# A selective scan whose partitions hold pairs of channels by states, with scaled copies read straight from PSUM and one buffer per pair

## The chip, the cores and the metric

The kernel runs on one core of one Trainium2 chip. The time is the device time of that core in microseconds: 16271.34 is the median of three runs before the change, which lie between 16253.17 and 16275.21. TensorE, VectorE, ScalarE and GpSimd are called PE, DVE, ACT and POOL in the profile, and SP is the engine from whose queue every DMA of this kernel is issued.

## What is computed

Two images of 256 x 256 pixels with 128 channels go through two layers, each of which adds its result to its input. The first is a group norm and an attention along one image axis with an output projection. The second, where nearly all of the change lies, is a group norm and a selective scan over the L = 65536 pixels of an image, for 256 inner channels d and 16 states n:

```python
xz = x @ in_proj_w.T;  xi, z = split(xz)           # 256 channels each
xs = silu(depthwise_conv3x3(xi))                   # (B, 256, L)
dts, Bs, Cs = rows of einsum(xs, x_proj_w)         # 8, 16 and 16 rows
delta = softplus(dt_w @ dts + dt_b);  A = -exp(A_logs)
h[d, n] = exp(delta[d] * A[d, n]) * h[d, n] + (delta[d] * xs[d]) * Bs[n]   # along L
y[d] = sum over n of h[d, n] * Cs[n]  +  Ds[d] * xs[d]
out = (layernorm(y) * silu(z)) @ out_proj_w.T
```

All data are float32.

## The kernel before the change

The attention runs first and writes its result `x1` to DRAM. Then comes the scan, in 128 steps: 64 for each image, each of four rows of pixels, so T = 1024 positions. Within a step a *unit* is one scan instruction on 128 partitions and 1024 positions. The 128 partitions are 32 channels by 4 states, so 256 channels by 16 states are 32 units (`NU = 32`). The partition of channel c and state r is 4c + r. `PAIRS` lists the 16 pairs of units in their order as half h of the channels, group m of four states, and first channel group q.

A unit needs four things. Its decay is `exp(delta * A)` on ACT (line 1237), where `delta_r` is a spread of 32 rows of delta over the 128 partitions, read back from DRAM (`spread`, line 1154; five buffers). Its drive is `du * B` on POOL, for the two units of a pair in one instruction of 2048 elements (line 1244), from `du_r`, another spread (two buffers), and `bb`, four rows of B repeated over the channels (`repeat`, line 1149). Its scan is on DVE (line 1275). After it, the last column is kept as the state for the next step (`remember`, lines 1282 and 1284, ACT), the result is multiplied by `cc`, the repeated C, and the sums over states are matmuls with the 0/1 matrix `sel` (`add_up`, line 1325). The multiplication is on DVE for 16 units (`product`, line 1292) and on POOL for the eight pairs in `POOLED` (`products`, line 1297).

The eight units of the last group of states (m = 3, `TURNED`) get their drive in another way. PE transposes delta times xs so that positions are on partitions (`turn_du`, line 965, into the PSUM tile `ut_ps`), ACT copies this into `zt` (`turn_du_out`, line 972, two of the eight blocks of 128 positions at a time), then makes the four states' versions of it by copies scaled by B (`drives`, line 976), and PE transposes each unit's 128 columns back (`turn_in`, line 1263) into PSUM. `zt` is laid out as block, channel, state: the fourth state's place takes the unscaled copy, every copy steps over four floats as it reads and writes, and the fourth is scaled in place and last.

PSUM has two buffers for decays, `da0` and `da1`, two banks for the running sums y, and two single banks, called p and f, through which pass all projections of the next step and the closing rows of the last one. SBUF has six buffers `work0` to `work5` of 2 x 1024 per partition, called rooms. A pair in `POOLED`, or of the turned ones, holds a room from its drive to its sum. For a pair whose products are on DVE, the drive's room is given back after the scan, and the product takes another (`work`, `open_pair`, `product`). The decay goes to PSUM, or, for turned units, to the room.

The order is written out by hand. `TIMES` gives each piece of work a time in units of a scan, relative to its step, and `at` and `at_time` collect the pieces of all steps, sort them by time and issue them so. The times only order: each engine runs its instructions in that order, and an instruction waits for those it depends on. The projections of a step carry times from about -47 on, more than one step ahead of its scans, and its closing rows (`finish_row`) up to 71. SP's queue, with the fetches, is ordered in the same way. A DMA that waits for a buffer holds up those behind it.

Of the kernel before, what the change touches and what calls it, by code (L numbers as in the profile page):

```python
# [22 lines left out]
def attn_then_ssm_kernel(  # L23
# [86 lines left out]
    for k in range(2):  # L110
# [37 lines left out]
    NQ = P // CQ  # L148
    NCG = DI // CQ
# [4 lines left out]
        sel, ident.rearrange("p (c r) -> p c r", r=SR), AX.X, ALU.add  # L154
# [4 lines left out]
    with tc.tile_pool(name="prep", bufs=1) as prep, tc.tile_pool(  # L159
# [30 lines left out]
        alog_d = dram.tile([CQ, SR, NCG, NSG], F32, name="alog_d")  # L190
        for g in range(NCG):
            for m in range(NSG):
                nc.sync.dma_start(
                    out=alog_d[:, :, g, m],
                    in_=A_logs[g * CQ : (g + 1) * CQ, m * SR : (m + 1) * SR],
                )
        alog = prep.tile([P, NCG, NSG], F32, name="alog")
        nc.sync.dma_start(out=alog, in_=alog_d.rearrange("c r g m -> (c r) g m"))
# [119 lines left out]
    with ExitStack() as actx:  # L318
# [268 lines left out]
        with tc.manual_schedule(engines=engines):  # L587
# [71 lines left out]
    POOLED = (2, 4, 10, 12, 18, 20, 26, 30)  # L659
    SUMS = ((0, 2), (4, 6), (8, 10), (12, 14), (16, 18), (20, 22), (24, 26), (28, 30))  # L660
    TIMES = {
        "add_up": (6.724, 10.523, 15.234, 17.357, 23.577, 27.066, 31.528, 34.187,),
        "begin": (-46.647,),
        "conv": (-37.319, -33.26, -30.256, -23.187,),
        "conv_out": (-37.203, -32.298, -29.079, -22.531,),
        "decay": (
            -0.457, -0.009, 1.46, 2.524, 2.97, 3.951, 4.748, 6.603, 7.256, 7.99, 7.7, 8.96, 9.084,
            7.786, 12.346, 13.841, 15.488, 16.811, 17.403, 14.296, 19.264, 20.338, 21.36, 21.952,
            23.923, 24.277, 25.955, 26.637, 26.688, 28.054, 29.215, 30.729,
        ),  # L670
        "drive": (
            -2.478, -0.654, 1.762, 3.81, 6.989, 11.716, 14.121, 17.755, 19.949, 23.283, 25.806,
            26.998,
        ),
        "drives": (
            -8.898, -8.755, 2.16, 8.854, -5.671, -4.828, -5.842, -1.931, -5.258, 3.165, -5.885,
            6.474, 2.13, 5.925, -3.57, 1.156,
        ),
        "fetch_b": (-4.274, -3.132, 4.233, 5.726, 22.495,),
        "fetch_c": (-2.23, 2.972, 5.721, 10.592, 28.034,),  # L680
        "fetch_cx": (-6.513,),
        "fetch_delta": (-9.068, -2.243, 0.347, -2.618, 11.064, 13.651, 5.759, 10.856,),
        "fetch_du": (-5.916, -3.021, 10.561, 13.429,),
        "gate": (-33.667, -30.07, -30.491, -26.072,),
        "gate_out": (-33.279, -28.439, -30.401, -25.691,),
        "inner": (-40.499, -39.775, -36.487, -34.84, -31.681, -31.179, -27.674, -24.89,),
        "inner_out": (-39.934, -39.214, -35.665, -34.411, -31.186, -30.784, -27.39, -23.412,),
        "load": (-52.341,),
        "normalise": (-43.293, -42.071,),
        "product": (  # L690
            0.814, 1.744, 6.726, 7.428, 8.79, 9.803, 15.226, 15.302, 17.41, 17.593, 23.225,
            23.505, 24.863, 25.246, 28.32, 29.93,
        ),
        "products": (5.397, 7.89, 14.546, 17.263, 21.546, 22.117, 27.902, 34.092,),
        "remember": (
            1.264, 2.345, 3.214, 6.053, 6.484, 7.988, 9.009, 9.1, 11.486, 14.169, 14.492, 15.761,
            17.254, 17.474, 20.057, 21.886, 23.549, 23.215, 25.088, 26.351, 27.149, 29.047,
            30.658, 32.752,
        ),
        "row_back": (41.992, 49.875, 57.857, 65.191,),  # L700
        "row_fetch": (43.062, 45.977, 52.544, 63.797,),
        "row_gated": (44.51, 49.95, 58.115, 65.232,),
        "row_leave": (45.329, 51.392, 61.182, 70.675,),
        "row_mix": (44.946, 51.011, 60.158, 69.774,),
        "row_norm": (41.251, 49.16, 55.004, 63.737,),
        "row_scales": (41.007, 47.422, 54.441, 63.428,),
        "row_stats": (39.857, 46.949, 53.374, 62.217,),
        "row_turn": (39.103, 45.623, 53.215, 61.229,),
        "silu": (-20.93,),
        "size": (-17.158, -16.246, -14.523, -14.865,),  # L710
        "size_out": (-16.533, -15.379, -13.973, -14.754,),
        "softplus": (-12.917,),
        "start_up": (-5.227, 19.105,),
        "start_up_y": (6.598, 23.449,),
        "states": (-20.725, -18.696,),
        "states_out": (-19.252, -17.616,),
        "times": (-11.031,),
        "turn": (-44.119, -42.473,),
        "turn_b": (-13.925,),
        "turn_b_out": (-12.571,),  # L720
        "turn_du": (-9.691, -6.021, -7.213, -4.676,),
        "turn_du_out": (-9.002, -5.843, -7.087, -4.562,),
        "turn_in": (9.374, 10.415, 10.881, 11.321, 17.974, 18.627, 19.701, 20.235,),
        "y_out": (20.647, 36.827,),
# [17 lines left out]
    LAST = TIMES["y_out"][NH - 1] + 0.1  # L742
# [23 lines left out]
    for i, piece in enumerate(pieces):  # L766
        at_time(i - 2.5, piece)

    def project(k):
# [23 lines left out]
        def begin():  # L793
            if s == 0:
                if k > 0:
                    nc.gpsimd.memset(xn[:, 0, :], 0.0)
                first = s1.tile([P, WT, C], F32, name="ob")
                nc.sync.dma_start(
                    out=first, in_=x1[b][0].rearrange("(t p) c -> p t c", p=P)
                )  # L800
# [624 lines left out]
```

## Time and profile before

| what | value |
|---|---|
| median of three runs | 16271.34 us |
| time of the profiled execution | 16262.75 us |
| its span, first to last instruction | 16261.0 us |
| mean granted PE clock | 0.926 |
| busy: PE, DVE, ACT, POOL | 84%, 84%, 85%, 78% |
| one step, from the 128 starts of silu (2550.3 to 16050.2 us) | 106.3 us |
| bytes moved by DMA | 3122 MB, 54.5% of the 16 DMA engines' span on the main queue |
| issues of `delta_r` and of `du_r` | 1024 each, of 512 KB, landing in 6.2 and 6.3 us |

A row of the groups reads: line, engine, operation, output and inputs by the program's names, shapes, count; then busy time in us and the mean of one in ns; then how long the engine was idle just before, and what ended that. A row of waits reads: who waited for whom, us in all, how many times, the longest. A row of the table of stretches gives, for a stretch of time, the busy time of every engine, the granted PE clock, the share of DMA and GB/s. A `SPq` row of the timeline is the issue of a DMA: its start, and how long SP took to issue it.

### The profile page before, as it was taken

To read this page: it belongs to the slowest core of one execution; us is meant where nothing else is said; L and a number is where in the kernel's file an instruction comes from. 1 tells how busy PE (TensorE), PEld (TensorE's weight loads), DVE (VectorE), ACT (ScalarE), POOL (GpSimd) and SP (SyncE) were. 2 spreads that over 40 slices of the span, in tenths; PEclk is the share of its full clock that TensorE was granted. 3 is DMA by queue.
4 is the path that set the end of the run, shared out by engine and by line. 5 is a ranking of instruction groups with operands and counts; after the bars stand their busy time and mean duration, and the time that the engine had idled before them with its cause. 6 is when DMAs were issued, how large, how long until landed. Compare 5 with 4: busy or idle time off the path is not lost.

```text
span 16261.0 us, 265160 instructions
## 1 busy us (share of the span) xinstructions
PE 13681.8 (84%) x102443; PEld 8025.9 (49%) x102443; DVE 13663.5 (84%) x11479; ACT 13899.9 (85%) x24467; POOL 12670.3 (78%) x2960
## 2 busy tenths in 40 slices
PE   6999997888888888888888888888888888888887
PEld 5877884444444444444444444444444444444444
DVE  6665556888888888888888888888888888888888
ACT  3555557999999999999999999999999999999997
POOL 1111115999999999989899999999999989999988
PEclk9999998999999999999999999999999999999998
DMA  4322224565655666555666556665556566566664
GB/s 189 135 84 88 84 83 153 209 213 206 212 209 207 212 213 208 208 206 209 211 208 211 209 205 213 213 209 207 207 208 216 202 209 209 208 212 208 212 209 168
DMA packets 1336402, 3122.11 MB, mean 192 GB/s; under 512 B 108856, under 2 KB 700256, under 8 KB 1314656
## 3 DMA queue, kind: packets, MB, share of 16 engines
q1 hardware_dynamic: 1335136, 3105.15, 54.5%
q8 instruction: 804, 13.17, 0.3%
q14 instruction: 462, 3.78, 0.1%
HBM read 2416.88 MB, written 687.88 MB: 191 GB/s over the span
## 4 chain that ended last, share of the span: by engine, by line
ACT 44%; PE 24%; DVE 8%; issue 5%; DMA 1%; POOL 1%; SPq 0%; POOLq 0%; DVEq 0%; ACTq 0%
ACT zt L976 14%; ACT da L1237 10%; DVE work L1275 7%; PE y L1325 5%; PE u_ps L851 4%; PE dt_ps L916 4%; ACT work L1237 3%; ACT raw L844 3%; ACT zt L972 3%; PE o_ps L1104 2%; PE da L1263 2%; PE xi_ps L835 2%; ACT sz L891 2%; PE yt L1053 2%; PE xd_ps L898 1%
## 5 line engine op out<-in xcount | busy, mean ns | idle before, releaser
L1244 POOL TENSOR_TENSOR work<-du_r,bb 128x2048 f32<-128x2048 f32 x1536 | 7163.3, 4679 | 793.6 <-DVE da L1275 409.9
L1275 DVE TENSOR_TENSOR_SCAN da<-da,state,work 128x1024 f32<-128x1024 f32 x2048 | 4776.2, 2344 | 256.2 <-ACT da L1237 216.9
L1237 ACT ACTIVATE da<-delta_r,a_neg 128x1024 f32<-128x1024 f32 x3072 | 3430.6, 1119 | 82.0 <-DVE work L1275 47.4
L976 ACT ACTIVATE zt<-zt,bt 128x256 f32<-128x256 f32 x4096 | 3073.1, 787 | 37.6
L1292 DVE TENSOR_TENSOR work<-da,cc 128x1024 f32<-128x1024 f32 x2048 | 2465.1, 1219 | 495.7 <-ACT state L1282 261.4
L1275 DVE TENSOR_TENSOR_SCAN work<-da,state,work 128x1024 f32<-128x1024 f32 x1024 | 2388.8, 2343 | 478.8 <-ACT da L1237 469.7
L1297 POOL TENSOR_TENSOR work<-work,cc 128x2048 f32<-128x2048 f32 x512 | 2350.9, 4592 | 419.0 <-ACT state L1284 415.0
L851 PE MATMUL u_ps<-raw,w_cv 128*32 128x255 f32 (+1 forms) x24576 | 1819.8, 456 | 896.3 <-ACT raw L844 337.4
L1275 DVE TENSOR_TENSOR_SCAN work<-work,state,da 128x1024 f32<-128x1024 f32 x1024 | 2346.4, 2333 | 158.0 <-PE da L1263 132.6
L1297 POOL TENSOR_TENSOR work<-work,ccx 128x2048 f32<-128x2048 f32 x512 | 2318.3, 4552 | 19.1 <-ACT state L1284 17.8
L1325 PE MATMUL y<-work,sel 128*32 128x512 f32 x16384 | 2204.0, 641 | 15.0 <-POOL work L1297 15.0
L851 PEld LDWEIGHTS u_ps<-raw,w_cv 128*32 128x32 f32 x24576 | 864.8, 128 | 1867.3 <-ACT sz L891 434.9
L475 POOL TENSOR_TENSOR x1g<-xc,bo_all 128x512 f32<-128x512 f32 x256 | 316.2, 1276 | 1843.9 <-DVE stats L530 1835.8
L835 PE MATMUL xi_ps<-xn,w_in 128*32 128x256 f32 x16384 | 1164.9, 392 | 342.9 <-ACT raw L844 325.9
L425 ACT ACTIVATE e<-s_ps,nmx 128x256 f32<-128x256 f32 x1024 | 477.2, 476 | 970.1 <-DVE nmx L416 877.0
L1263 PE MATMUL da<-ident,zt 128*128 128x128 f32 x8192 | 1179.0, 291 | 25.5 <-ACT state L1282 22.0
L1237 ACT ACTIVATE work<-delta_r,a_neg 128x1024 f32<-128x1024 f32 x1024 | 1163.4, 1148 | 2.0 <-PE y L1325 0.3
L1325 PEld LDWEIGHTS y<-work,sel 128*32 128x32 f32 x16384 | 561.7, 115 | 1208.4 <-issue 1059.0
L1263 PEld LDWEIGHTS da<-ident,zt 128*128 128x128 f32 x8192 | 975.9, 149 | 326.1 <-DVE work L1275 107.5
L1053 PE MATMUL yt<-centre,ys 128*128 128x256 f32 x4096 | 1010.5, 390 | 127.3 <-ACT ob L1121 127.2
L835 PEld LDWEIGHTS xi_ps<-xn,w_in 128*32 128x32 f32 x16384 | 500.3, 111 | 1025.2 <-ACT raw L844 504.1
L1053 PEld LDWEIGHTS yt<-centre,ys 128*128 128x128 f32 x4096 | 738.2, 190 | 477.8 <-ACT ob L1121 285.8
(175 smaller groups left out, 22878.7 us busy)
## 6 DMA issues: line engine op xcount, KB each, us to landing
delta_r<-delta_d SPq DMA_DIRECT2D x1024, 512.0 KB, 6.2
du_r<-du_d SPq DMA_DIRECT2D x1024, 512.0 KB, 6.3
bb<-bc_d SPq DMA_DIRECT2D x640, 512.0 KB, 6.8
cc<-bc_d SPq DMA_DIRECT2D x640, 512.0 KB, 4.7
sz_d<-sz SPq DMA_DIRECT2D x128, 1024.0 KB, 4.1
xs_d<-xs SPq DMA_DIRECT2D x128, 1024.0 KB, 7.5
delta_d<-sz SPq DMA_DIRECT2D x128, 1024.0 KB, 5.0
du_d<-xs SPq DMA_DIRECT2D x128, 1024.0 KB, 6.2
```

The lines of the kernel that those rows point to most:

```text
L835: nc.tensor.matmul(o["xi", j][r * CQ : (r + 1) * CQ, q, :], w_in[:, h, c : c + CQ], xn[:, i * RB + r, :], start=True, stop=True,)
L851: nc.tensor.matmul(o["u"][q * CQ : (q + 1) * CQ, r, a:z], w_cv[:, h * NQ + q, r, dx, :], o["xin"][:, q, a + dx - 1 : z + dx - 1], start=(i ...
L916: nc.tensor.matmul(o["dt"], w_dt[:, h, :], o["xd"][0:DR, i * TB : (i + 1) * TB], start=True, stop=True,)
L976: nc.scalar.activation(v["zt"][:, j, :, r], v["zt"][:, j, :, SR - 1], AF.Copy, scale=v["bt"][:, j, r : r + 1],)
L1053: nc.tensor.matmul(o["yt"][:, j, :], ys[k, h][:, t0 + j * P : t0 + (j + 1) * P], centre[:, (1 - h) * P : (1 - h) * P + DI], start=(h == 0) ...
L1237: nc.scalar.activation(da, spreads["delta", k, h, q], AF.Exp, scale=a_neg[:, g, m : m + 1])
L1244: nc.gpsimd.tensor_tensor(open_pair(t, time_of(k, "drive", DRIVEN.index(t % NU))), spreads["du", k, h, q], repeat_of("bb", t).unsqueeze(1) ...
L1263: nc.tensor.transpose(da[:, j * P : (j + 1) * P], given[k]["zt"][:, j, a : a + CQ, :].rearrange("p c r -> p (c r)"), ident,)
L1275: nc.vector.tensor_tensor_scan(u["h"], u[ins[0]], u[ins[1]], st, ALU.mult, ALU.add)
L1292: nc.vector.tensor_tensor(u["yc"], u["h"], repeat_of("cc", t), ALU.mult)
L1297: nc.gpsimd.tensor_tensor(hb, hb, repeat_of("cc", t).unsqueeze(1).to_broadcast([P, 2, T]), ALU.mult)
L1325: nc.tensor.matmul(y[q * CQ : (q + 1) * CQ, cols], sel, units[u]["yc"][:, cols], start=False, stop=last,)
```

## The change

Five things change together.

- The partitions of a unit: channel c = 2a + b and state r now lie on partition 8a + 2r + b, so that two neighbouring channels are neighbours (`CB = 2`). `sel`, `a_neg`, the repeats of B and C and `zt` follow. `zt` becomes block, pair of channels, state, channel of the pair. The small DRAM tile `bc_d` holds each row of B and C twice.
- A spread becomes two transfers, one for even and one for odd partitions, of 64 partitions each.
- `turn_du_out` goes. `drives` reads `ut_ps` in PSUM, for all four states, and writes pairs of floats into `zt`.
- A pair keeps one room from its drive (or decay) to its sum; the DVE product overwrites the drive.
- Unit 30's product and state no longer go with unit 31's on POOL: 31 is multiplied on DVE (17 products in place of 16), 30 on POOL alone (`single`).

Beside that, the gating multiply of a closing row is issued in two halves, the first row of an image is normalised after the others, the group scales of the second image are computed ahead of the first step, the closing rows of the last step are ordered one unit later, and every time in `TIMES` is new.

```diff
-        sel, ident.rearrange("p (c r) -> p c r", r=SR), AX.X, ALU.add
+        sel.rearrange("p (a b) -> p a b", b=CB),
+        ident.rearrange("p (a r b) -> p a b r", r=SR, b=CB),
+        AX.X,
+        ALU.add,
...
-    POOLED = (2, 4, 10, 12, 18, 20, 26, 30)
+    POOLED = (2, 4, 10, 12, 18, 20, 26)
+    SINGLES = (30,)
...
         "drive": (
-            -2.478, -0.654, 1.762, 3.81, 6.989, 11.716, 14.121, 17.755, 19.949, 23.283, 25.806,
-            26.998,
+            -0.913, -0.273, 0.924, 3.225, 7.461, 10.178, 10.839, 19.277, 21.727, 16.814, 25.326,
+            27.843,
         ),
         "drives": (
-            -8.898, -8.755, 2.16, 8.854, -5.671, -4.828, -5.842, -1.931, -5.258, 3.165, -5.885,
-            6.474, 2.13, 5.925, -3.57, 1.156,
+            -9.769, -9.422, -8.809, -9.524, -7.004, -6.997, -6.999, -7.229, -5.886, -3.425,
+            -5.126, -5.754, -4.723, -4.106, -3.106, -2.068,
         ),
...
-        "fetch_delta": (-9.068, -2.243, 0.347, -2.618, 11.064, 13.651, 5.759, 10.856,),
-        "fetch_du": (-5.916, -3.021, 10.561, 13.429,),
+        "fetch_delta": (-2.633, -1.452, -1.361, -10.151, 10.962, 10.988, 10.844, 15.649,),
+        "fetch_du": (-4.933, -1.787, 10.579, 10.708,),
...
-                v["bc"] = dr.tile([2 * NS, T], F32, name="bc_d")
+                v["bc"] = dr.tile([2 * NS, CB, T], F32, name="bc_d")
...
-        def turn_du_out(i):
-            if i == 0:
-                v["zt"] = s6.tile([P, T // P, DI, SR], F32, name="zt")
-            nc.scalar.copy(v["zt"][:, 2 * i : 2 * i + 2, :, SR - 1], o["ut", i])
-
         def drives(j, n, m):
+            if (j, n) == (0, 0):
+                v["zt"] = s6.tile([P, T // P, DI // CB, SR, CB], F32, name="zt")
             for r in range(n, m):
                 nc.scalar.activation(
-                    v["zt"][:, j, :, r],
-                    v["zt"][:, j, :, SR - 1],
+                    v["zt"][:, j, :, r, :],
+                    o["ut", j // 2][:, j % 2, :].rearrange("p (a b) -> p a b", b=CB),
                     AF.Copy,
                     scale=v["bt"][:, j, r : r + 1],
                 )
...
     def spread(k, name, tl, h, q):
-        nc.sync.dma_start(
-            out=tl,
-            in_=given[k][name][h, q * CQ : (q + 1) * CQ, :]
-            .unsqueeze(1)
-            .to_broadcast([CQ, SR, T]),
-        )
+        rows = given[k][name][h, q * CQ : (q + 1) * CQ, :]
+        for j in range(CB):
+            nc.sync.dma_start(
+                out=tl[j:P:CB, :],
+                in_=rows[j:CQ:CB, :].unsqueeze(1).to_broadcast([CA, SR, T]),
+            )
...
-            hb = work(now, summed(t) if pooled(t) else t + 1)
+            hb = work(now, done(t))
             for i in range(2):
-                units[t + i].update({"pair": hb, "hb": hb[:, i, :], "yc": hb[:, i, :]})
+                units[t + i].update({"pair": hb, "hb": hb[:, i, :]})
...
     def product(t):
         u = units[t]
-        if t % 2 == 0:
-            yc = work(time_of(t // NU, "product", KEPT.index(t % NU)), summed(t))
-            for i in range(2):
-                units[t + i]["yc"] = yc[:, i, :]
-        nc.vector.tensor_tensor(u["yc"], u["h"], repeat_of("cc", t), ALU.mult)
+        nc.vector.tensor_tensor(u["hb"], u["h"], repeat_of("cc", t), ALU.mult)
+
+    def single(t):
+        u = units[t]
+        nc.gpsimd.tensor_tensor(u["hb"], u["h"], repeat_of("cc", t), ALU.mult)
```

## The prediction

> **What bounds the kernel now.** I read the page first (every working engine is 78 to 85% busy, so no share names the limit), then the silu rows (line 871), to get one step of the scan loop: its 128 executions start from 2550.3 to 16050.2 us, so a step is (16050.2 - 2550.3) / 127 = 106.3 us, and 128 steps are 13,606 of the 16,261 us span. The attention ahead and the ramps are not changed in anything that counts.
>
> Then busy time in stretches of one step, cut where silu runs (8062) and where the next step's copies begin (8104.3):
>
> ```profile
> core 0: us, PE busy (x) PEld busy (x) DVE busy (x) ACT busy (x) POOL busy (x), PEclk, DMA share, GB/s
> 7998.00:8062.00 64.00, 50.66 (x494) 25.69 (x492) 55.85 (x32) 62.03 (x107) 56.52 (x14) 0.95 0.55 187
> 8062.00:8104.30 42.30, 38.41 (x204) 22.47 (x204) 39.05 (x22) 36.18 (x59) 40.27 (x9) 0.88 0.71 244
> ```
>
> The step has two stages. In the first (64 us) ScalarE is busy 62.03 us and nothing else is over 57: it is the bound. In the second (42.3 us) POOL, DVE and PE are each over 90%, and ScalarE is not. The chain that ended last says the same: from 8034 to 8062 it is ScalarE pieces and their issue alone, many of them of `zt`; after that DVE, then mostly PE.
>
> What VectorE waits for in the first stage:
>
> ```profile
> DVE work L1275 <- ACT da L1237: 3.7, 3, 1.6
> DVE work L1292 <- ACT state L1282: 2.0, 2, 1.5
> DVE da L1275 <- ACT da L1237: 1.6, 2, 1.4
> DVE work L1292 <- DMA cc<-bc_d: 0.5, 1, 0.5
> ```
>
> 7.3 of its 8.15 idle us there end with a ScalarE instruction: the decays and state copies stand behind the `zt` copies in ScalarE's queue. The groups that the change touches:
>
> ```profile
> L1244 POOL TENSOR_TENSOR work<-du_r,bb 128x2048 f32<-128x2048 f32 x1536 | 7163.3, 4679 | 793.6 <-DVE da L1275 409.9
> ...
> L976 ACT ACTIVATE zt<-zt,bt 128x256 f32<-128x256 f32 x4096 | 3073.1, 787 | 37.6
> L1292 DVE TENSOR_TENSOR work<-da,cc 128x1024 f32<-128x1024 f32 x2048 | 2465.1, 1219 | 495.7 <-ACT state L1282 261.4
> ...
> L844 ACT COPY raw<-xi_ps 128x512 f32<-128x512 f32 x1024 | 597.4, 583 | 57.1 <-PE xi_ps L835 51.7
> ...
> L972 ACT COPY zt<-ut_ps 128x512 f32<-128x512 f32 x512 | 550.2, 1075 | 113.5 <-PE ut_ps L965 113.5
> ...
> L1077 ACT ACTIVATE yn<-yt,rstd 128x256 f32<-128x256 f32 x1020 | 425.2, 473 | 0.1
> ...
> L1096 DVE TENSOR_TENSOR yn<-yd,szr 128x512 f32<-128x512 f32 x510 | 343.7, 674 | 167.5 <-PE yd L1088 167.5
> ```
>
> Of these, L976 is 32 and L972 four copies a step: 25.2 + 4.3 = 29.5 us of ScalarE, nearly all in the first stage.
>
> **The change, part by part (us per step).**
>
> *Scaled copies from PSUM, in pairs of channels.* The four copies out of `ut_ps` (L972) go: -4.3. The 32 scaled copies stay, but read contiguous PSUM and write runs of two floats. No row has such a write. Nearest is L1077, the same copy from PSUM with a scale per partition, contiguous: 473 ns. The dearest is a write of single floats 16 bytes apart: L972 against L844, both 512 elements, shows 1075 - 583 = 492 ns more, so 246 for 256 elements: 473 + 246 = 719. Between them: the copies of 1024 (L1335, 1007) and 512 elements (583) give 159 ns fixed and 0.83 per element, so L972's 512 separate writes take (1075 - 159) / 512 = 1.79 each; 128 runs at 1.79 are 229 ns where 256 contiguous elements are 212. That gives 490 ns, and I take it: 32 x (787 - 490) = -9.5. At 719 it would be -2.2, at 473 -10.0. [...]
>
> The bank of `ut_ps` is now held through eight copies (about 4 us by the 490) in place of one of 1.08. Behind it wait the next projections of PE on that bank; PE is busy 50.66 of 64 us there, and this cover takes it. If it did not, some 3 us on each of four turns would stand on PE, and the conv behind them would be late.
>
> *17 products on VectorE.* One product of 1219 ns more, +1.2. The gating multiply is cut in two: 674 ns for 512 and 1219 for 1024 elements give 129 ns fixed, so four more instructions are +0.5. POOL loses half a product of 4592 ns (L1297's row): -2.3. One state copy more on ScalarE, under 0.2.
>
> *One room per pair.* The product is written over the drive's room, so a room is held from the drive to the summing matmuls, not in two shorter holds. Counting holds over the written times, 4.2 of 6 rooms were in use on average and 4.6 will be. POOL's drives wait 410 us in all for a scan to free a room (3.2 a step); that wait turns into one for PE's summing. I put it at 0, because the tightest new hand-over (the drive for unit 16 after the summing of units 4 to 7) has another drive of 4.7 us of POOL ahead of it, while the summing is 16 matmuls (1.7 to 2.5 us where the chain has them). Without that cover it is at most those 2.5.
>
> *Spreads in two transfers.* 16 spreads become 32: 16 DMAs of about 0.55 us of issue on SP, +8.8. SP issued 48 a step in 106 us, so it has the room; what counts is where it stands in order. The trace of the queue:
>
> ```profile
> 8013.26 1.24 SPq L1155 DMA_DIRECT2D du_r<-du_d  x2
> 8021.70 0.38 SPq L1122 DMA_DIRECT2D out_dram<-ob  x1
> 8022.13 1.16 SPq L1155 DMA_DIRECT2D delta_r<-delta_d  x2
> ```
>
> Two `du_r` issues of 1.2 us become four of 2.3, and the `delta_r` behind them start 1.1 to 1.7 later. [...] Who waits: the decays of units 0 to 2 of the next step, issued behind `du_r`, which waits for POOL's last drive. From the end of that drive POOL still does one product and one drive (4.6 + 4.7) before unit 0 can scan, and unit 1 follows 2.34 later, so its decay (1.12) must start at 10.5; SP needs 6 issues (3.5) and 6.2 to land, 9.7. It fits by 0.8 us. Price 0, up to 6 if serialized.
>
> *Everything reordered by the new times.* By these, ScalarE's copies are ended before unit 0 scans and no longer run into units 1 to 8; silu and softplus keep their places beside the turned units. PE's work by stage is the same within 1 us. The group scales of the second image move ahead of the first step, a few us once, beside a load that PE waits for anyway.
>
> **The sum.** First stage: ScalarE falls from 62.0 to 48.2 and VectorE becomes the longest: 55.85 + 1.5 = 57.4 (POOL 56.5 - 2.3). Of its idle time the 7.3 us owed to ScalarE shrink; with ScalarE at some 80% and two decay buffers I leave 1.5, and 0.8 of others: 59.7 for 64.0. Second stage: nothing of its limits is touched, 42.3. Together 102.0, or 4.3 less. Times 128 is 550 us. The profiled execution took 16,262.75 (span 16,261.0), so 15,713; the median of the runs is 8.6 higher: 15,720. A difference under 0.2%, 33 us, could not be told from none.
>
> Own range of this case: with no wait left on ScalarE and DVE at its busy time, and the second stage's POOL work (40.3) with 1.4 of its waits: 58.2 + 41.7 = 99.9, 15,450; with pairs at 719 ns ScalarE still has 55.5 and about half of the waits stay, 104, 15,980.
>
> **Rivals.**
> - *Only the slack moves* (0.14). DVE and POOL wait for each other through rooms and landed halves, and the step keeps some 105: 1.0 to 1.5 a step, 16,090. For it: POOL and DVE sum to 94 and 96 of busy time per step, and today the best engine is 8% under the step. Against: the trace puts the first stage's waits on ScalarE.
> - *The split fetches come late* (0.13, slower). Place: `delta_r` behind four `du_r` on SP, twice a step. If a half lands in 10 us in place of 6.2, the decay is 3 us late each time, and ScalarE's queue behind it too. It decides when lateness is above 4.3 a step; at 10 us for both places it is 6 a step: 108.0, or 1.7 over today's, 16,490. For it: POOL already waits 155 us for `du_r`. Against: ScalarE waits 1.4 us for `delta_r` in the whole run.
> - *The pairs don't speed the copy and VectorE takes what is freed* (0.04): within 0.2%, 16,270.
>
> **Chances.** The main case 0.69, own range 15,450 to 15,980; with the first rival, faster 0.83, same 0.04, slower 0.13. The range from 15,450 to 16,110 leaves out the slow cases, that of no difference, and a little below: under 2 in 10.
>
> **What would show it.** Right: the group of scaled copies from PSUM near 490 ns, no copy row of 512 elements into `zt`; the step near 102; ScalarE near 83 us a step; VectorE's waits for decays and state copies under a third of today's 948 us (469.7 + 216.9 + 261.4 in the whole run). Wrong: `delta_r` or `du_r` among the releasers of decays and drives with over 2 us a step; PE's projections waiting for `zt` copies; copies near 719.

## The result, and the profile after

The changed kernel takes 17,068.77 us (median of four runs, 17,059.38 to 17,074.62), the kernel before 16,262.26 beside it: a ratio of 1.0495, 95% interval 1.0477 to 1.0513. It is 4.95% slower; forecast were 15,720, within 15,450 to 16,110. The profiled execution has a span of 17,064.4 us. A step, from the silu executions on `sz` (2574.0 to 16,856.8 us), is (16,856.8 - 2574.0) / 127 = 112.5 us for 106.3.

From the page of the kernel after: busy times, the main DMA queue (packets, MB, share of the 16 DMA engines' span), the chain that ended last by engine and by line, three groups, and DMA issues with KB and median us from issue to landing. The chain by engine on the page of the kernel before, for comparison, stands first.

```profile
ACT 44%; PE 24%; DVE 8%; issue 5%; DMA 1%; POOL 1%; SPq 0%; POOLq 0%; DVEq 0%; ACTq 0%
```

```profile
PE 13801.8 (81%) x102443; PEld 7769.8 (46%) x102443; DVE 13797.9 (81%) x12119; ACT 12254.1 (72%) x24083; POOL 12369.2 (72%) x2960
...
q1 hardware_dynamic: 1376608, 3122.06, 65.3%
...
DMA 27%; PE 24%; ACT 13%; DVE 7%; POOL 7%; issue 6%; SPq 1%; DVEq 0%; POOLq 0%; ACTq 0%
DMA cc<-bc_d 9%; PE y L1331 8%; DMA sz_d<-sz 7%; DMA du_r<-du_d 7%; POOL work L1250 6%; DVE da L1281 3%; PE dt_ps L927 3%; PE xi_ps L843 3%; DMA xr<-xs_d 3%; DVE work L1294 2%; PE y L1320 2%; PE u_ps L859 2%; ACT da L1243 2%; ACT L770 2%; DVE work L1281 1%
...
L1250 POOL TENSOR_TENSOR work<-du_r,bb 128x2048 f32<-128x2048 f32 x1536 | 7161.5, 4673 | 2071.9 <-PE y L1331 1053.6
L1294 DVE TENSOR_TENSOR work<-da,cc 128x1024 f32<-128x1024 f32 x2176 | 2613.8, 1216 | 678.9 <-DMA cc<-bc_d 651.3
L984 ACT ACTIVATE zt<-ut_ps,bt 128x256 f32<-128x256 f32 x4096 | 1654.2, 515 | 3.7 <-PE ut_ps L976 3.7
...
delta_r<-delta_d SPq DMA_DIRECT2D x2048, 256.0 KB, 7.9
du_r<-du_d SPq DMA_DIRECT2D x2048, 256.0 KB, 6.1
bb<-bc_d SPq DMA_DIRECT2D x640, 512.0 KB, 7.6
cc<-bc_d SPq DMA_DIRECT2D x640, 512.0 KB, 6.7
sz_d<-sz SPq DMA_DIRECT2D x128, 1024.0 KB, 9.8
```

ScalarE gave what was forecast of it: copies of 515 ns, and (13,899.9 - 12,254.1) / 128 = 12.9 us less a step for 13.8 (62.0 - 48.2). But ScalarE has left the chain (13% for 44%), and DMA has entered it (27% for 1%). The queue moves nearly the same bytes as before (3122 MB for 3105), yet its packets take 0.653 x 17,064 = 11,143 us of 16 engines for 0.545 x 16,261 = 8862, a quarter more.

The stretches of one step (columns as in those shown of before). Since the copies and silu have moved against the scans, the cuts are put at scans: from the scan of unit 20 to that of unit 7 of the next step, and on to unit 20. The prediction's cuts of the kernel before lie within 3 us of these scans.

```profile
7986.20:8047.40 61.20, 49.57 (x467) 24.02 (x469) 54.32 (x33) 46.17 (x97) 56.09 (x14) 0.90 0.75 192
8047.40:8095.50 48.10, 39.88 (x244) 21.64 (x240) 40.85 (x26) 38.38 (x65) 38.11 (x9) 0.93 0.72 223
```

In the first stage ScalarE has fallen to 46.17 us of work (48.2 were forecast), yet the stage takes 61.2 us where 59.7 were forecast. The second has grown from some 43 us to 48.1, and PE, DVE and POOL are 79 to 85% busy in it where each was over 90%. The waits say for what; the last of these rows is of the kernel before:

```profile
POOL work L1250 <- PE y L1331: 1053.6, 333, 7.8
DVE work L1294 <- DMA cc<-bc_d: 651.3, 127, 6.5
...
ACT sz L938 <- DMA sz_d<-sz: 529.9, 126, 5.8
...
POOL work L1250 <- DMA du_r<-du_d: 330.4, 112, 15.7
POOL work L1250 <- DMA delta_r<-delta_d: 288.8, 49, 6.7
ACT da L1243 <- DMA delta_r<-delta_d: 266.3, 191, 3.8
```

```profile
DVE work L1292 <- DMA cc<-bc_d: 171.2, 114, 5.3
```

Waits put down to `du_r` and `delta_r` hold up POOL and ACT for 885 us, 6.9 a step; the prediction had put its sign of failure at 2. (POOL's drives do not read `delta_r`, so its row of 288.8 us may stand for another fetch; without it there are 4.7 a step.) And `cc`, which the change to the spreads doesn't touch, holds up DVE for 651 (171 before). One kind of transfer has got slower for all.

### The profile page after: what moved, and what is told of

Its sections match the earlier page's. It is cut to its first block, busy times and chain, and to the rows that moved or that the text cites. A ratio compares the mean times of both kernels' runs of the same rounds, so it can differ in the third digit from the quotient of the medians.

```text
span 17064.4 us, 269148 instructions
## 1 busy us (share of the span) xinstructions
PE 13801.8 (81%) x102443; PEld 7769.8 (46%) x102443; DVE 13797.9 (81%) x12119; ACT 12254.1 (72%) x24083; POOL 12369.2 (72%) x2960
## 4 chain that ended last, share of the span: by engine, by line
DMA 27%; PE 24%; ACT 13%; DVE 7%; POOL 7%; issue 6%; SPq 1%; DVEq 0%; POOLq 0%; ACTq 0%
DMA cc<-bc_d 9%; PE y L1331 8%; DMA sz_d<-sz 7%; DMA du_r<-du_d 7%; POOL work L1250 6%; DVE da L1281 3%; PE dt_ps L927 3%; PE xi_ps L843 3%; DMA xr<-xs_d 3%; DVE work L1294 2%; PE y L1320 2%; PE u_ps L859 2%; ACT da L1243 2%; ACT L770 2%; DVE work L1281 1%
## 5 line engine op out<-in xcount | busy, mean ns | idle before, releaser
L1281 DVE TENSOR_TENSOR_SCAN da<-da,state,work 128x1024 f32<-128x1024 f32 x2176 | 5059.8, 2344 | 1128.6 <-ACT da L1243 538.1
L1294 DVE TENSOR_TENSOR work<-da,cc 128x1024 f32<-128x1024 f32 x2176 | 2613.8, 1216 | 678.9 <-DMA cc<-bc_d 651.3
L1331 PE MATMUL y<-work,sel 128*32 128x512 f32 x16384 | 2676.4, 783 | 23.0 <-POOL work L1303 16.1
L1281 DVE TENSOR_TENSOR_SCAN work<-da,state,work 128x1024 f32<-128x1024 f32 x896 | 2074.4, 2339 | 144.3 <-ACT da L1243 125.5
L1303 POOL TENSOR_TENSOR work<-work,cc 128x2048 f32<-128x2048 f32 x384 | 1757.6, 4577 | 136.6 <-ACT state L1290 136.5
L984 ACT ACTIVATE zt<-ut_ps,bt 128x256 f32<-128x256 f32 x4096 | 1654.2, 515 | 3.7 <-PE ut_ps L976 3.7
L859 PE MATMUL u_ps<-raw,w_cv 128*32 128x255 f32 (+1 forms) x24576 | 1486.9, 391 | 40.3 <-ACT sz L899 13.5
L927 PE MATMUL dt_ps<-xr,w_dt 8*128 8x512 f32 x1024 | 740.6, 810 | 626.1 <-ACT state L1288 431.2
L976 PE MATMUL ut_ps<-ident,xs 128*128 128x128 f32 x2048 | 389.7, 322 | 933.8 <-DVE yn L1104 422.7
L859 PEld LDWEIGHTS u_ps<-raw,w_cv 128*32 128x32 f32 x24576 | 771.9, 113 | 784.4 <-ACT zt L984 151.5
```

The costliest lines, as they stand in the source:

```text
L859: nc.tensor.matmul(o["u"][q * CQ : (q + 1) * CQ, r, a:z], w_cv[:, h * NQ + q, r, dx, :], o["xin"][:, q, a + dx - 1 : z + dx - 1], start=(i ...
L927: nc.tensor.matmul(o["dt"], w_dt[:, h, :], o["xd"][0:DR, i * TB : (i + 1) * TB], start=True, stop=True,)
L984: nc.scalar.activation(v["zt"][:, j, :, r, :], o["ut", j // 2][:, j % 2, :].rearrange("p (a b) -> p a b", b=CB), AF.Copy, scale=v["bt"][:, ...
L1281: nc.vector.tensor_tensor_scan(u["h"], u[ins[0]], u[ins[1]], st, ALU.mult, ALU.add)
L1294: nc.vector.tensor_tensor(u["hb"], u["h"], repeat_of("cc", t), ALU.mult)
L1303: nc.gpsimd.tensor_tensor(hb, hb, repeat_of("cc", t).unsqueeze(1).to_broadcast([P, 2, T]), ALU.mult)
```

## The experiments

Of two readings, the first is that a spread in two transfers is late because there are more transfers, or because of where they stand in SP's order. The second is that something in the form of the transfers makes each packet slower. A number from the packet records of the traces tells these apart: every run moves 606,208 packets of 4096 bytes, some 442,000 of which are spreads and repeats. Their mean time was 183 ns before and 236 after. Runs of different groups have kernels before of 16,262 to 16,293 us beside them, so they are compared to 0.2% at best.

### One transfer again, and two of other shapes

In a1, a4 and b1 each partition of a spread gets another channel's delta and `du`, so they are of use for their time alone; a2 and a3 give every partition what the kernel before does.

a1, the changed kernel with spreads in one transfer:

```diff
-        rows = given[k][name][h, q * CQ : (q + 1) * CQ, :]
-        for j in range(CB):
-            nc.sync.dma_start(
-                out=tl[j:P:CB, :],
-                in_=rows[j:CQ:CB, :].unsqueeze(1).to_broadcast([CA, SR, T]),
-            )
+        nc.sync.dma_start(
+            out=tl,
+            in_=given[k][name][h, q * CQ : (q + 1) * CQ, :]
+            .unsqueeze(1)
+            .to_broadcast([CQ, SR, T]),
+        )
```

> The changed kernel with each spread as one transfer of 128 partitions, as before the change (each partition then gets the delta and du of another channel, so this is for time alone). Stride theory (partitions two apart make each packet slower) and number theory (32 transfers in place of 16 fill the queue): 15,650 to 15,950, mean time of the 4096-byte packets back from 236 to about 185 ns. Order theory (the new times and the one room per pair keep the engines waiting, the transfers only show it): 16,900 to 17,070.

15,904.75, ratio 0.9751 (0.972 to 0.9781), packets 206 ns: the split of the spreads costs 1164 us of the changed kernel. The packets come only a little more than half of the way back to 183, so something else slows them too.

a2, the kernel before in two transfers, each of all 32 rows for two of the four states; a3, the same in two halves of 16 rows; a4, the changed kernel in two halves; b1, the changed kernel with the form of a2:

```diff
 a2, b1
+        for j in range(2):
+            nc.sync.dma_start(
+                out=tl[j:P:2, :],
+                in_=rows.unsqueeze(1).to_broadcast([CQ, SR // 2, T]),
+            )
 a3, a4
+        for j in range(2):
+            nc.sync.dma_start(
+                out=tl[j * P // 2 : (j + 1) * P // 2, :],
+                in_=rows[j * CQ // 2 : (j + 1) * CQ // 2, :]
+                .unsqueeze(1)
+                .to_broadcast([CQ // 2, SR, T]),
+            )
```

> The kernel before with each spread in two transfers, one for even and one for odd partitions; results unchanged. Stride theory: slower, 16,700 to 17,300, and the 4096-byte packets go from 183 to about 235 ns. Number theory: slower by as much. Order theory: within 100 us of 16,262.

> The kernel before with each spread in two transfers of partitions 0 to 63 and 64 to 127; results unchanged. Stride theory: nearly as before, 16,250 to 16,450, packets near 185 ns. Number theory: like the strided split, 16,700 to 17,300. Order theory: within 100 us of 16,262.

> The changed kernel with each spread in two transfers of partitions 0 to 63 and 64 to 127 (each partition then gets another channel's delta and du, for time alone). Stride theory: 15,700 to 16,100. Number theory: 17,000 to 17,100, as the changed kernel. Order theory: the same 17,000 to 17,100.

> The changed kernel with the split that cost the kernel before only 17 us: each of the two transfers of a spread reads all 32 rows and writes each to two partitions, in place of 16 rows to four (each partition then gets another channel's delta and du, for time alone). Number and order theory (twice the transfers behind the short leads of the new order): 16,950 to 17,150, as the changed kernel. Pattern theory (it is what a transfer reads and where it writes): 15,900 to 16,300, as with one transfer.

a2: 16,302.95, ratio 1.0012 (1.0001 to 1.0022), 186 ns. a3: 16,485.42, 1.0107 (1.0072 to 1.0142), 217 ns. a4: 17,388.94, 1.0661 (1.0628 to 1.0693), 250 ns. b1: 16,008.72, 0.9834 (0.9815 to 0.9854), 206 ns. So b1 has just as many transfers as the changed kernel, in the same order of issue, and is 1060 us faster; two transfers for one cost 104 us (b1 less a1), a tenth of what was lost. The number of transfers falls as the main cause, and with it the late start behind the issues of `du_r`. The stride of the partitions falls too: a2 writes every second partition and is not slower, and a4, which does not, is slower than the changed kernel. With the order alone, a1 would have stayed near 17,000. Of the theories named so far, only that of the pattern, what a transfer reads and where it writes, is left.

b2 is the kernel before with the changed kernel's split (again other channels, for time alone), and d1 the changed kernel with three fetches of delta put behind the stores of `sz_d` and `xs_d` in SP's order, since ACT waits for `sz_d`:

```diff
 b2
+                out=tl[j:P:2, :],
+                in_=rows[j:CQ:2, :].unsqueeze(1).to_broadcast([CQ // 2, SR, T]),
 d1
-        "fetch_delta": (-2.633, -1.452, -1.361, -10.151, 10.962, 10.988, 10.844, 15.649,),
+        "fetch_delta": (-2.633, -1.452, -1.361, -10.151, 11.31, 11.33, 11.29, 15.649,),
```

> The kernel before with the spreads of the changed kernel, two transfers of 16 rows, one to even and one to odd partitions (each partition then gets another channel's delta and du, for time alone). Number and order theory: 16,250 to 16,380, as with the other split in this order. Pattern theory: 16,700 or more.

> The changed kernel with three fetches of delta (times 10.844, 10.962, 10.988) set to 11.29 to 11.33, so that SP issues the two stores of silu, sz_d and xs_d, ahead of these six transfers. Number and order theory: the wait of ScalarE for sz_d (530 us in all) falls under 150 us and the time is 16,400 to 16,900. Pattern theory: within 100 us of 17,069.

b2: 16,444.84, 1.0102 (1.0082 to 1.0122), 209 ns. Its two largest waits for fetches:

```profile
POOL work L1244 <- DMA du_r<-du_d: 453.8, 182, 5.3
DVE work L1292 <- DMA cc<-bc_d: 438.1, 132, 8.0
```

The packets are as slow as the pattern theory has it, but the time is not, 16,445 for 16,700 or more: the same slow transfers cost the kernel before 1% and the changed one some 7%. In b2, POOL and DVE wait 566 us more for `du_r` and `cc` than before, and the time shows 170 of them; the rest takes the place of other waits. Why the new kernel can't do the same is not shown. Its leads are one candidate, and they are mixed: counted from the traces, waits included, the median from a fetch's issue to its first use is 16.8 us before and 11.7 in c1 (a version with the new order, below) for `delta_r`, 11.5 and 9.6 for `du_r`, but 8.6 and 10.9 for `cc`. The other is that ScalarE bounds the first stage of the kernel before and leaves the others slack; no run parts the two. d1: 17,102.87, 1.0506 (1.0485 to 1.0527). `sz_d` lands in 5.7 us for 9.8, and ACT no longer waits for it, but its decays of turned units now wait 603 us for `delta_r` (43 in the changed kernel). This change of order moves the lateness and doesn't mend it.

### The change without its layout of partitions

c1 keeps three of the five parts, copies straight from PSUM in pairs, one room and 17 products, and the new order. It takes back the partition order, the split of the spreads and the doubled `bc_d`. To have pairs all the same, the two channels of a pair are c and c + 128, one of each half h:

```diff
-                v["zt"] = s6.tile([P, T // P, DI // CB, SR, CB], F32, name="zt")
+                v["zt"] = s6.tile([P, T // P, P, SR, NH], F32, name="zt")
...
-                        o["ut", i][:, j, h * P : (h + 1) * P], o["xs"][:, h, t : t + P], ident
+                        o["ut", i][:, j, :, h], o["xs"][:, h, t : t + P], ident
...
-                given[k]["zt"][:, j, a : a + CA].rearrange("p a r b -> p (a r b)"),
+                given[k]["zt"][:, j, q * CQ : (q + 1) * CQ, :, h].rearrange("p c r -> p (c r)"),
```

> The changed kernel with the partitions and the single spreads of before, and still pairs of floats in zt: a pair is a channel and the channel 128 above it, the transposes into ut_ps write every second float, and the transposes out of zt read every second column. Results as the reference's. Number and order theory: 15,800 to 16,000, as with one transfer in the changed kernel (15,905). If the order of the new times were itself the cause: 16,900 or more. If TensorE's strided loads cost much: the transposes into da over 400 ns in place of 279, and 16,000 to 16,400.

15,582.34 (15,574.43 to 15,600.13), 0.9573 (0.9557 to 0.9589): 4.3% faster than before and 8.7% faster than the changed kernel. It beats both. Its page:

```profile
PE 13280.7 (85%) x102443; PEld 7810.3 (50%) x102443; DVE 13763.1 (88%) x12119; ACT 12305.8 (79%) x24083; POOL 12365.0 (79%) x2960
...
q1 hardware_dynamic: 1335136, 3105.15, 56.3%
...
PE 38%; DVE 19%; ACT 12%; DMA 8%; issue 6%; POOL 1%; SPq 0%; DVEq 0%; ACTq 0%; POOLq 0%
...
L1242 POOL TENSOR_TENSOR work<-du_r,bb 128x2048 f32<-128x2048 f32 x1536 | 7168.0, 4683 | 771.9 <-PE y L1322 750.2
...
L1285 DVE TENSOR_TENSOR work<-da,cc 128x1024 f32<-128x1024 f32 x2176 | 2602.1, 1216 | 27.3 <-ACT state L1279 0.7
...
L977 ACT ACTIVATE zt<-ut_ps,bt 128x256 f32<-128x256 f32 x4096 | 1664.2, 514 | 3.8 <-PE ut_ps L969 3.7
```

One of its first stages, by the same scans:

```profile
7949.80:8005.20 55.40, 46.01 (x460) 23.20 (x456) 54.12 (x33) 46.44 (x96) 55.40 (x14) 0.94 0.59 205
```

The wait for `cc` is gone (27 us idle ahead of the products for 679), DMA is 8% of the chain, and a step, from the first and last of softplus's 128 executions on `sz` (2562.5 and 15,409.0), is 101.2 us. The rest of the change is thus worth 693 us (16,275 beside it), some more than the 550 forecast. By stages, as means over 88 steps in us, cut at the scans of units 20, 7 and 20:

| | first | second | step |
|---|---|---|---|
| before | 63.6 | 42.9 | 106.5 |
| forecast | 59.7 | 42.3 | 102.0 |
| c1 | 55.7 | 45.5 | 101.2 |
| changed kernel | 62.4 | 50.3 | 112.8 |

f1 and f2 each put one part of the change back into c1, the doubled repeats and the split of the spreads; f3 takes the pairs from c1 (`zt` as before the change, single floats four apart, but still straight from PSUM):

```diff
 f1
+                v["bc"] = dr.tile([2 * NS, 2, T], F32, name="bc_d")
...
+        rows = given[k]["bc"][a : a + SR].rearrange("r b t -> (r b) t")
+        nc.sync.dma_start(out=tl, in_=rows.partition_broadcast(CQ // 2))
 f2
+        for j in range(2):
+            nc.sync.dma_start(
+                out=tl[j:P:2, :],
+                in_=rows[j:CQ:2, :].unsqueeze(1).to_broadcast([CQ // 2, SR, T]),
+            )
 f3
-                    v["zt"][:, j, :, r, :],
+                    v["zt"][:, j, :, r],
```

> The version with the two halves of the channels as pairs (15,582), with one part of the change put back: bc_d holds each row of B and C twice and a repeat reads eight rows and writes each to 16 partitions, in place of four rows to 32. Partitions get B and C of another state, so it is of use for its time alone. If this pattern of the repeats is what keeps the changed kernel with single spreads 320 us above: about 15,900, packets of 4096 bytes at 206 ns in place of 181, bb and cc landing in 7.6 to 7.8 us in place of 5.8 and 5.9. If those 320 us come from the layout of the pairs or the partition order: about 15,580, packets at 181.

> The same version, with the change's split of the spreads put back: two transfers, each reads every second row, four times, and writes every second partition. The channels go to other partitions, so it is of use for its time alone. If the split's pattern costs what it cost in the changed kernel: 1,000 to 1,200 us more, 16,600 to 16,800, 4 KB packets above 205 ns. If it costs much only together with the doubled repeats: under 400 more, below 15,980.

> The same version, but zt as before (channel, state) and the scaled copies, straight from PSUM for all four states, write single floats with a step of four in place of pairs. By the prediction's upper bound the copy takes 719 ns in place of 514, so ScalarE has 6.6 us more a step in the first stage; that stage was to be 2 us longer, 15,840. If ScalarE is no longer what anything waits for: within 50 us of 15,582. If the copies cost 1075 ns as those of the kernel before did, ScalarE has 18 us more and the step is back above 106: 16,200 or more.

f1: 15,881.74, 0.976 (0.9745 to 0.9774), 206 ns. f2: 16,589.44, 1.0197 (1.0182 to 1.0212), 210 ns. So of the 1486 us between c1 and the changed kernel, the split takes 1007 and the doubled repeats 299, and 180 are left. a1 and f1 have the same transfers and differ in the layout of the pairs and the partitions, and are 23 us apart; so most of the 180 comes when split and doubled repeats are both there. f3: 16,056.70, 0.9872 (0.9856 to 0.9889). Its copies:

```profile
L977 ACT ACTIVATE zt<-ut_ps,bt 128x256 f32<-128x256 f32 x4096 | 2220.8, 739 | 4.5 <-PE ut_ps L969 4.1
```

The pairs are worth 225 ns a copy and 474 us in all, more than the 256 that the prediction's dear case gave (2 us a step); the other parts without them leave about 220.

### What in the transfer makes it slow

All on c1, each changing the spreads alone, and all but g4 with other channels, for time alone. `rows` are 32 rows of one group, or what the slice says:

```diff
 f4  two transfers as in f2, of adjacent rows
+                in_=rows[j * CQ // 2 : (j + 1) * CQ // 2, :].unsqueeze(1).to_broadcast([CQ // 2, SR, T]),
 f5  one transfer, 16 rows, each eight times in succession
+        nc.sync.dma_start(out=tl, in_=rows[0 : CQ // 2].unsqueeze(1).to_broadcast([CQ // 2, 2 * SR, T]))
 f6  one transfer, the same 16 rows in turns
+        nc.sync.dma_start(out=tl, in_=rows[0 : CQ // 2].partition_broadcast(2 * SR))
 g2  one transfer, four rows in turns
+        nc.sync.dma_start(out=tl, in_=rows[0:SR].partition_broadcast(CQ))
 g4  one transfer, the 32 rows, written as 16 pairs
+            in_=rows.rearrange("(a b) t -> a b t", b=2).unsqueeze(2).to_broadcast([CQ // 2, 2, SR, T]),
 g5 (n = 16), g6 (n = 32)  one transfer, all 128 rows of the half, once each
+        nc.sync.dma_start(out=tl, in_=given[k][name][h].rearrange("(i a) t -> a i t", a=n))
```

> The same version with spreads in two transfers to every second partition, but each reads 16 adjacent rows, four times each, in place of every second row; time alone, as the channels go to other partitions. If reading every second row (8 KB apart) is what slows the packets: as the single spread, 15,600 to 15,700 and about 185 ns a packet. If it is that a transfer has only 16 source rows, each read four times: as with every second row, within 100 us of that run and its packets too.

> The version with the halves as pairs, spreads again in one transfer of 128 partitions, but it reads only 16 rows and writes each to eight partitions next to each other; the partitions get other channels, so it is of use for its time alone. If a transfer is slow when it goes over 16 rows in place of 32, whatever the number of transfers: packets of 4096 bytes at 205 ns or more, landing above 7.5 us, time near that of the two transfers, 16,300 to 16,700. If it takes two transfers as well as 16 rows: near the single spread of 32 rows, 15,580 to 15,700, packets at 181 to 185 ns.

> The same 16 rows in one transfer of 128 partitions, but in turns: all 16 rows, then all 16 again, eight times over, as the repeats of four rows are read 32 times over; time alone, for the same reason. If it is the few source rows that slow a transfer: as the run that writes each of 16 rows eight times in succession, within 60 us. If it is the order in which rows and copies are gone through: clearly different from it, and near 15,580 to 15,700 if that one is slow.

> The same version; each spread reads only four rows, in turns, 32 times over, as the repeats do, so the outermost count is 32 and the source rows are fewer than in any other run; the partitions get other channels, so it is of use for its time alone. If the way in which 16 engines share the partitions sets the packets' time: 15,560 to 15,650, packets at 178 to 185 ns. If few source rows slow a transfer: worse than the run with 16 rows eight times each, above 17,000.

> The version with the halves as pairs; each spread reads the same 32 rows in the same order into the same partitions in one transfer, only written down as 16 pairs of two rows, four times each, so that the transfer's outermost count is 16 in place of 32. [...] If the source rows or their number make them slow, or nothing but the data counts: 15,560 to 15,620 and 181 ns.

> The version with the halves as pairs; each spread reads all 128 rows of its half, every row once, as 16 groups of eight rows that lie 16 apart: the outermost count is 16. The partitions get other channels, so it is of use for its time alone. If the outermost count of a transfer (how the DMA engines share the partitions) sets the packets' time: 205 to 240 ns a packet, 16,400 to 17,300. If it is that few rows are read many times: about 15,580 and 181 ns.

> The same 128 rows, each once, into the same partitions, as 32 groups of four rows that lie 32 apart: the outermost count is 32; time alone. If the outermost count sets the packets' time: 178 to 186 ns a packet and 15,520 to 15,650. If the rows, their number or their distance set it: as the run with 16 groups, within 100 us.

f4, 16,657.70, 1.0234 (1.0219 to 1.025): adjacent rows are as slow as every second one, so the distance of the rows isn't it. f5, 17,136.21, 1.0523 (1.0505 to 1.0541): one transfer is slower still than two. f6, 20,534.84, 1.2611 (1.2592 to 1.2629): the same rows in another order, and 3400 us more. g2, 15,523.55, 0.9534 (0.952 to 0.9548): four rows only, and fast, so few rows read often isn't it either. g4, 15,625.49, 0.9588 (0.9572 to 0.9605), tells nothing of this, as the two counts are joined to one of 32 again in the built program; it is c1 a second time, and 0.3% from it. g5 and g6 settle it: the same 128 rows, the same partitions, one transfer, grouped by 16 or by 32. (Which row goes to which partition differs with it: rows read one after the other lie 16 or 32 rows apart. That distance isn't it, as f5, where it is 0 or 1, has packets as slow as g5.) 17,165.13, 1.0538 (1.0522 to 1.0554), against 15,571.34, 0.9566 (0.9549 to 0.9583). From g5's page, the main queue and the spreads' landing, then from g6's:

```profile
q1 hardware_dynamic: 1335136, 3105.15, 62.8%
...
delta_r<-delta_d SPq DMA_DIRECT2D x1024, 512.0 KB, 10.7
du_r<-du_d SPq DMA_DIRECT2D x1024, 512.0 KB, 7.1
```

```profile
q1 hardware_dynamic: 1335136, 3105.15, 56.7%
...
delta_r<-delta_d SPq DMA_DIRECT2D x1024, 512.0 KB, 6.8
du_r<-du_d SPq DMA_DIRECT2D x1024, 512.0 KB, 5.5
```

Same packets, same bytes, 10.7 us for 6.8. All runs in one table, by the outermost count of the transfer's source (the first of the counts that its access pattern goes through in the built program); shares are of the 606,208 packets of 4096 bytes:

| run | spreads | repeats | mean ns | under 170 ns | 280 to 350 ns | us |
|---|---|---|---|---|---|---|
| before | 32 | 32 | 183 | 84% | 4% | 16,262 |
| a2 (order of before) | 2 x 32 | 32 | 186 | 83% | 4% | 16,303 |
| f3 | 32 | 32 | 184 | 86% | 3% | 16,057 |
| c1 | 32 | 32 | 181 | 86% | 2% | 15,582 |
| g4 | 32 | 32 | 181 | 86% | 2% | 15,625 |
| g6 | 32 | 32 | 181 | 87% | 2% | 15,571 |
| g2 | 32 | 32 | 181 | 87% | 2% | 15,524 |
| f1 | 32 | 16 | 206 | 63% | 16% | 15,882 |
| a1 | 32 | 16 | 206 | 63% | 17% | 15,905 |
| b1 | 2 x 32 | 16 | 206 | 65% | 16% | 16,009 |
| b2 (order of before) | 2 x 16 | 32 | 209 | 52% | 9% | 16,445 |
| f2 | 2 x 16 | 32 | 210 | 50% | 6% | 16,589 |
| f4 | 2 x 16 | 32 | 213 | 47% | 7% | 16,658 |
| a3 (order of before) | 2 x 16 | 32 | 217 | 49% | 19% | 16,485 |
| f5 | 16 | 32 | 230 | 44% | 25% | 17,136 |
| g5 | 16 | 32 | 230 | 44% | 25% | 17,165 |
| d1 | 2 x 16 | 16 | 235 | 29% | 23% | 17,103 |
| after | 2 x 16 | 16 | 236 | 28% | 22% | 17,069 |
| a4 | 2 x 16 | 16 | 250 | 27% | 39% | 17,389 |
| f6 | 8 | 32 | 235 | 48% | 20% | 20,535 |

There is no exception: with 32 everywhere the packets take 181 to 186 ns, and with 16 anywhere 206 or more. Counts of spreads and repeats other than 8, 16 and 32 were not run.

f6 has a second loss: its packets take 235 ns, near f5's 230, yet it takes 3400 us more. In its trace exactly eight packets of 4096 bytes are under way during 36% of the time from 5000 to 11,000 us (1.1% in c1, which has 16 for 27%). f6 is the only run with a count of 8; what ties the eight packets to it no run shows.

Why 16 is slow where 32 is fast is not shown either, since the packet records name no engine and no partition: that the engines' shares of the partitions are behind it, as the expectations of g2 and g5 have it, was the author's supposition. What the records show is the packets' times. The median where all counts are 32 is 159 ns, and a1, f1, f5 and g5 have a second heap at 280 to 350, with 16 to 25% of the packets; twice the median is 318. In the changed kernel, with its even and odd halves, most of the slow packets lie between 170 and 280 ns (47% of all), so one doubling does not describe them all.

## Why the prediction was wrong

- **Where it failed: "Spreads in two transfers … Price 0, up to 6 if serialized".** They cost 1007 us on c1, 7.9 a step, and 1164 in the changed kernel. The step reasoned about the start of the transfers (1.1 to 1.7 us later) and took the landing of 6.2 us as given. But the rows of the page that land in 6.0 to 6.3 us, of 64 KB (`bc_d`), 128 KB (`xres`) and 512 KB (`delta_r`), all had another form than the new ones, and that page had rows of 512 KB from 4.7 us (`cc`) to 6.8 (`bb`); that the form of a transfer sets the time of its packets was in no part of the working. Nor did it ask what slower packets do to the others on the same 16 engines: DVE waits 480 us more for `cc` than before.
- **A term left out.** The doubled `bc_d` is named in the change, and the sum has no term for it. It turned the repeats from an outermost count of 32 to one of 16, and cost 299 us.
- **"Up to 6 if serialized"** is a term that no run shows. In its place, the first transfers of `delta_r` and `du_r` in the changed kernel land in 8.2 and 5.8 us (medians from issue to landing), the second in 7.8 and 6.2, where the whole spreads of before took 6.2 and 6.3. Two transfers of 32 groups cost 0.1% in the old order (a2) and some 100 us in the new one (b1 less a1). What costs is the count in each.
- **"It fits by 0.8 us"** was the right place to look, and rested on a landing of 6.2 us. With the 7.9 of the changed kernel the same sum gives 3.5 + 7.9 = 11.4 us for 10.5, and ACT's decays do wait 266 us for `delta_r`. It looked at this one fetch alone; `cc`, `du_r` and `sz_d` are waited for longer.
- **Scaled copies: right.** Taken 490 ns, measured 515 (514 in c1); the upper bound of 719 was measured, with single floats, at 739. The row it went by (1075 ns for 512 single floats four apart, 583 for 512 contiguous) pointed the right way: single floats four apart cost 225 of f3's 739 ns. The held bank: in c1 PE's matmuls wait 190 us for `zt` copies in the whole run (175 of them those of the next turn, 12 the conv), where before they waited 460, so the price of 0 held.
- **17 products, gating halves: not tested alone.** DVE's busy time rose by (13,797.9 - 13,663.5) / 128 = 1.05 us a step for 1.7 forecast, POOL's fell by 2.35 for 2.3.
- **One room per pair: priced 0, and c1 agrees.** The wait for a scan did turn into one for PE's summing, and it is not small (750 us in c1), but the idle time ahead of POOL's drives is 772 us in c1 and was 794. In the changed kernel it is 2072, with the late fetches; the room alone was not undone.
- **The sum.** Without the transfers' forms the step is 101.2 for 102.0 forecast, and the total 15,582 for 15,720, inside the case's own range. That it comes so close is in part luck, as two errors cancel: the first stage fell by 7.9 us for 4.3, and the second, "42.3" and "nothing of its limits is touched", grew by 2.6; why is open. VectorE, forecast as the longest of the first stage, has 54.12 us in the stretch of c1 shown, and POOL all 55.40. And VectorE's waits for decays and state copies, which were to fall under a third of 948 us, are 541 in c1 (one of them 80 us long) and 1158 in the changed kernel.
- **The rivals.** "The split fetches come late" had the sign, and with 16,490 and 108.0 a step comes close to f2 (16,589, and 108.9 from softplus at 2565.7 and 16,398.5), in part by chance, since its landing of 10 us was not met: `delta_r` lands in 7.7 there. Its place was wrong: not `delta_r` behind four issues of `du_r`, for b1 has those too. Its chance of 0.13 was too low for a new form of transfer that no row of the trace showed.

## What to carry to other kernels

Before a transfer is split or its source doubled, write down the counts that its access pattern goes through, and compare them with those of a transfer in the trace that is fast; a form that no row shows needs a bound of its own, however small its bytes. Price a slower packet at all who wait for transfers (in b2, where only the spreads changed, DVE waits 438 us for `cc`, 171 before), and in the new kernel, not in the old one, where the same split cost a sixth (170 us in b2, 1007 in f2). Where a layout serves two ends (pairs for a copy, partitions for a transfer), look for one that serves the first without touching the second, as the two halves of the channels did here.

## What was not expected of the hardware

- A transfer's grouping alone, with the same rows, partitions and bytes, moved its packets from 181 to 230 ns and its landing from 6.8 to 10.7 us (g6, g5). With eight groups, exactly eight packets are under way for 36% of the time (f6).
- 16 groups of eight partitions in one transfer (f5, 17,136) are slower than two transfers of 16 groups of four (f4, 16,658); why is open.
- Reading four rows in place of 32 may have given a little (g2, 0.9534 against c1's 0.9573, where c1 run a second time, g4, has 0.9588); no run explains it.
- The pairs of c1 are read back with a step of two floats, and PE's weight loads of `zt` take 209 ns for 142 with single floats (f3). It costs nothing that the time shows: f1, with 209 ns, takes 15,882, and a1, with 145 and the same transfers, 15,905.
- The granted PE clock is lower in the longer of these runs: 0.845 in f6 (20,535 us), 0.902 in g5 (17,165), 0.907 in the changed kernel (17,069), 0.926 before (16,262), 0.955 in g6 (15,571). That more waiting brings the lower clock is not shown. The summing matmuls do not follow this clock alone: their mean is 783 ns in the changed kernel, 683 in c1 (0.952) and 641 before.
